# A list scheduler's table of priorities: own rows for odd quads in the middle and for the last quad

## The chip, the cores and the metric

The kernel runs on one core of one Trainium2 chip. The time is the device time in microseconds (us) of one execution. The kernel before takes 765.96 us (median of 3 runs, 761.38 to 770.71).

The engines are TensorE (PE in the profile; PEld is its weight load), VectorE (DVE), ScalarE (ACT), GpSimd (POOL) and SyncE (SP, which issues all the DMAs here). Each has a queue of its own and executes it in order. What one engine needs from another it waits for with semaphores.

## The reference

The input `x` is 128 sequences of 64 tokens of 256 numbers. One block of a hyperbolic transformer is applied to it, with a condition of 256 numbers for each sequence, and the input is added to the result:

```
ada = t_emb @ w_ada + b_ada                      # six rows of 256 for each sequence
sh_msa, sc_msa, g_msa, sh_mlp, sc_mlp, g_mlp = split(ada, 6)
xm  = expmap0(layer_norm(logmap0(x)) * (1 + sc_msa) + sh_msa)
q, k, v = plin(xm, w_q, b_q), plin(xm, w_k, b_k), plin(xm, w_v, b_v)   # to 16 heads of 16
out_h = expmap0(softmax(qt @ kt / sqrt(16)) @ vt)                      # qt = logmap0(q), ...
attn_t = g_msa * logmap0(plin(_from_heads(out_h), w_o, b_o))
x1  = mobius_add(x, expmap0(attn_t))
xm  = expmap0(layer_norm(logmap0(x1)) * (1 + sc_mlp) + sh_mlp)
ff  = plin(plin(xm, w_f1, b_f1), w_f2, b_f2)                           # 256 -> 1024 -> 256
return x + mobius_add(x1, expmap0(g_mlp * logmap0(ff)))
```

`plin(x, w, b)` is `expmap0(logmap0(x) @ w + b)`. `logmap0`, `expmap0` and `mobius_add` scale rows by factors made from norms and inner products of rows. All is float32.

## The kernel before

**Tiles and stages.** The 8192 tokens are 64 tiles of 128 rows (two sequences in each). Four tiles make a *quad*, and there are 16 quads, 0 to 15. They are worked in groups: quad 0 alone, then the pairs 1 and 2, 3 and 4, up to 13 and 14, then quad 15 alone. For each group the kernel goes through attention of its quads (`attention`, in two pairs of tiles a quad: `attention_pair`), the scalar factors of the Möbius addition (`scalars`), the inner sums and the second norm (`inner`), the MLP of its quads (`mlp`) and, a group later, the final sum and the store (`final`). The MLP has no activation function between its two matrices, so both are multiplied into one at the start (`wm`).

**Names that the prediction uses.** In attention: `yTa` are the transposed modulated rows, `fia` holds the inverse norms of a quad and `rTa` its transpose, which brings the bias into the projection; `usq` and `vsq` are squares of the projections, `qx` and `kT` transposed queries and keys, `pt` the exponentials. In the MLP: `n2s` and `n2o` are scale and shift of the second norm, `ym` the modulated rows (multiplied with `mdm` and summed with it, one half of a quad at a time), `yTm` their transpose, `fim` and `rTm` the inverse norms and their transpose, `iv` and `rTh` those of the second product; `p` is a gated product (`p<-bank,fh,gm`) and `jd` the discarded output of an inner product that is made beside it. `ja` is the discarded output of ScalarE's sums of squares. `bank` is one of the 8 banks of the matmul accumulator.

**The order is not the program's.** The code above only records operations. `Plan.add` (line 152) notes each with its engines (some may run on either of two), an estimated duration, what it reads and writes, and a *key*; `Plan.run` (line 209) then plays the machine: whenever an engine is free, it takes the operation with the smallest key among those whose inputs are there and whose buffers have room, and moves the estimated clock on. `Plan.issue` (line 381) emits the operations in that order, and the chip's queues execute what stands there. So the order of each engine's queue, the buffer that an operation gets and, where two engines are allowed, the engine are all decided by the keys and the estimates.

**The keys.** An operation's key is the number of its quad (plus 0.5 for the second half of an attention and for the group's scalars) plus an offset for its *stage*, a short name such as `qkv`, `rTa` or `mum`. The offsets stand in a table written out by hand, `pl.off`, in units of quads: -4 pulls a stage four quads ahead, 9 puts it off by nine. The stage's name gets a mark by the quad: `<` below key 3, `>` from key 13 on, none between them. A stage without an entry for its mark takes the one without a mark.

```
op.st = self.st + ("<" if self.key < self.early else ">" if self.key >= self.late else "")
op.key = (self.key + self.off.get(op.st, self.off.get(self.st, 0.0)), len(self.ops))
```

**Dummies and holds.** Where TensorE has nothing ready in the planner's clock, the planner puts a matmul of the identity with itself (`warm`, line 1373; line 1374 in the profile), which writes into a free bank that nobody reads. It does so only if TensorE's planned work in the last 2.6 us is at most `share` of them; `fill_occ`, 0.22 us, is what a dummy counts there. `hold` (line 1441) lets an engine leave a ready operation where it is, if one with a smaller key becomes ready within that many microseconds.

## Time and profile before

| | before |
|---|---|
| median of 3 runs | 765.96 us (761.38 to 770.71) |
| the profiled execution's time | 766.87 us |
| its span, first to last instruction | 765.1 us |
| mean granted TensorE clock | 0.986 |
| PE, DVE, ACT, POOL busy | 721.8, 656.1, 505.8, 122.7 us |
| read from and written to HBM | 77.89 MB, 9.18 MB |

The busy times are of one profiled execution, by engine. PE's includes the dummies of line 1374. A group of instructions is told by line, engine, operation and tiles; where a helper records every operation of a kind, all of them have its line (509 for matmuls, 516 for transposes, 449, 438 and 415 for VectorE, 492 for ScalarE), so the tiles tell them apart. Rows of stages have a stretch in us from the span's start, its length, the busy time and the number of instructions of PE, PEld, DVE, ACT and POOL, the granted clock, the busy share of the DMA engines and GB/s.

### The profile page before, as it was taken

Reading aid. Unit: us, or ns where it says so; the run is one execution under the profiler, and the core shown is the slowest. Engines: PE = TensorE matmul, PEld = TensorE weight load, DVE = VectorE, ACT = ScalarE, POOL = GpSimd, SP = SyncE. Lnnn points to the kernel's source line nnn. Section 1 sums busy time; section 2 is a strip of 40 time slices with the busy share of each in tenths; the row PEclk is TensorE's granted clock in tenths of the full one; section 3 lists DMA queues with packets and bytes.
Section 4 is the critical chain, followed back from the end, with each engine's and each line's share of the span. In section 5 each row is a group of like instructions: output and inputs, shape, how many; then the busy total and the mean of one; then the engine's idle time right before and its main releaser. Section 6 shows DMA issues by size and latency. Waiting matters only on the chain.

```text
span 765.1 us, 24046 instructions
## 1 busy us (share of the span) xinstructions
PE 721.8 (94%) x9170; PEld 513.1 (67%) x9170; DVE 656.1 (86%) x2870; ACT 505.8 (66%) x1599; POOL 122.7 (16%) x98
## 2 busy tenths in 40 slices
PE   7999999999999989998999989998999989998998
PEld 2546566676767666766867676766777666777778
DVE  6797899889987798969977898879995998989976
ACT  1345558466975879577775888487774877486453
POOL 0002102001220123002220223004310122004012
PEclk9999999999999999998899999999999999999999
DMA  5859835302560147312562157213651224126213
GB/s 157 264 146 243 192 89 152 102 29 85 146 159 30 44 126 220 90 65 74 165 165 70 57 139 201 77 57 105 169 170 30 71 73 139 56 57 159 91 45 123
DMA packets 74776, 88.63 MB, mean 116 GB/s; under 512 B 7186, under 2 KB 57630, under 8 KB 74660
## 3 DMA queue, kind: packets, MB, share of 16 engines
q1 hardware_dynamic: 74660, 87.09, 40.7%
q8 instruction: 72, 1.18, 0.7%
q14 instruction: 44, 0.36, 0.2%
HBM read 77.89 MB, written 9.18 MB: 114 GB/s over the span
## 4 chain that ended last, share of the span: by engine, by line
DVE 42%; PE 36%; ACT 10%; DMA 7%; issue 4%; POOL 1%; SPq 1%; DVEq 0%; POOLq 0%; ACTq 0%
PE bank L509 28%; ACT ja L492 6%; PE bank L516 5%; DVE x L449 5%; DVE jd L449 4%; DVE hs L464 3%; DVE u L438 3%; PE bank L1374 3%; DVE p L449 3%; DMA xp<-in_x_dram 2%; DMA mdm<-ada_d 2%; DMA gm<-ada_d 2%; DVE mxq L438 1%; ACT ym L428 1%; DVE ya L438 1%
## 5 line engine op out<-in xcount | busy, mean ns | idle before, releaser
L509 PE MATMUL bank<-wqkv,yTa 128*128 128x512 f32 (+1 forms) x512 | 177.5, 493 | 1.5 <-ACT pt L492 0.6
L509 PEld LDWEIGHTS bank<-wqkv,yTa 128*128 128x128 f32 x512 | 94.3, 191 | 72.1 <-issue 60.9
L509 PE MATMUL bank<-wm,yTm 128*128 128x256 f32 (+1 forms) x512 | 104.3, 356 | 0.5 <-DVE u L438 0.5
L509 PEld LDWEIGHTS bank<-wm,yTm 128*128 128x128 f32 x512 | 87.5, 190 | 18.8 <-issue 4.0
L441 POOL TENSOR_TENSOR x<-x,xr 128x512 f32<-128x512 f32 x31 | 40.4, 1320 | 297.4 <-ACT x L492 284.8
L1374 PE MATMUL bank<-ident 128*128 128x128 f32 x500 | 70.5, 290 | 3.0 <-ACT ja L492 1.1
L441 POOL TENSOR_TENSOR ya<-ya,mda 128x512 f32<-128x512 f32 x30 | 39.5, 1322 | 206.5 <-DMA ga<-ada_d 56.0
L509 PEld LDWEIGHTS bank<-ve,pt 64*64 64x64 f32 x4096 | 64.4, 137 | 11.2 <-issue 4.0
L492 ACT ACTIVATE pt<-bank 128x512 f32<-128x512 f32 x128 | 67.6, 606 | 5.5 <-PE bank L509 5.4
L1374 PEld LDWEIGHTS bank<-ident 128*128 128x128 f32 x500 | 63.3, 199 | 10.3 <-issue 3.7
L509 PE MATMUL bank<-ve,pt 64*64 64x17 f32 x4096 | 67.6, 209 | 0.1
L441 POOL TENSOR_TENSOR ym<-ym,mdm 128x512 f32<-128x512 f32 x31 | 42.1, 1368 | 133.6 <-DVE ym L438 48.2
L509 PE MATMUL bank<-wo,zT 128*128 128x256 f32 x256 | 60.5, 379 | 0.0
L509 PEld LDWEIGHTS bank<-wo,zT 128*128 128x128 f32 x256 | 46.2, 190 | 5.0
L492 ACT ACTIVATE qx<-bank,par 128x512 f32<-128x512 f32 x64 | 43.2, 686 | 9.1 <-PE bank L516 9.0
L516 PE MATMUL bank<-ident,u 128*128 128x128 f32 x256 | 38.7, 285 | 9.6 <-ACT pt L492 9.3
L492 ACT ACTIVATE ja<-x 128x256 f32<-128x256 f32 x64 | 26.7, 417 | 29.9 <-DVE x L449 28.9
L509 PEld LDWEIGHTS bank<-qx,kT 32*64 32x64 f32 x2048 | 32.1, 133 | 17.2 <-issue 5.6
L516 PEld LDWEIGHTS bank<-ident,u 128*128 128x128 f32 x256 | 29.2, 143 | 20.6 <-ACT pt L492 11.2
L509 PE MATMUL bank<-qx,kT 32*64 32x128 f32 x2048 | 40.4, 283 | 1.9 <-ACT qx L492 1.3
L438 DVE TENSOR_TENSOR u<-bank,g 128x512 f32<-128x512 f32 x64 | 41.5, 681 | 0.0
L449 DVE SCALAR_TENSOR_TENSOR p<-bank,fh,gm 128x256 f32<-128x256 f32 x64 | 28.1, 477 | 14.7 <-PE bank L509 11.0
(276 smaller groups left out, 1531.3 us busy)
## 6 DMA issues: line engine op xcount, KB each, us to landing
mdm<-ada_d SPq DMA_DIRECT2D x64, 256.0 KB
mda<-ada_d SPq DMA_DIRECT2D x60, 256.0 KB
x<-in_x_dram SPq DMA_DIRECT2D x16, 512.0 KB
ga<-ada_d SPq DMA_DIRECT2D x64, 128.0 KB
gm<-ada_d SPq DMA_DIRECT2D x64, 128.0 KB
xr<-in_x_dram SPq DMA_DIRECT2D x32, 256.0 KB
out_dram<-p SPq DMA_DIRECT2D x15, 512.0 KB
xp<-in_x_dram SPq DMA_DIRECT2D x26, 256.0 KB
```

The source lines that it names most:

```text
L428: fn2 = lambda: self.nc.scalar.activation(R(out), R(in0), AF.Identity, scale=R(s1), bias=R(s2))
L438: fn = lambda: self.nc.vector.tensor_tensor(R(out), R(a), R(b), op)
L441: fn2 = lambda: self.nc.gpsimd.tensor_tensor(R(out), R(a), R(b), op)
L449: fn = lambda: self.nc.vector.scalar_tensor_tensor(R(out), R(a), R(s), R(b), op0, op1, **({} if accum is None else {"accum_out": R(accum)}))
L464: fn = lambda: self.nc.vector.tensor_reduce(R(out), R(a), AX.X, ALU.add)
L492: fn = lambda: self.nc.scalar.activation(R(out), R(a), func, scale=R(scale), **{k: R(v) for k, v in kw.items()})
L509: fn = lambda: self.nc.tensor.matmul(R(out), lhsT=R(lhsT), rhs=R(rhs), start=start, stop=stop, skip_group_check=onto)
L516: fn = lambda: self.nc.tensor.matmul(R(out), lhsT=R(a), rhs=ident, start=start, stop=True, is_transpose=True, skip_group_check=not start)
L1374: nc.tensor.matmul(place[:, 0:P], lhsT=ident, rhs=ident, start=True, stop=True)
```

## The change

The marks become five. Below key 3 it is still `<`. Between 3 and 13, a key whose quad is odd (3, 5, 7, 9, 11, and their halves) gets `+`; an even one has none. From 13 to 15 it is `>`, and from 15 on, the last quad, `!`. The table of offsets is written anew as a whole, with rows for the new marks; the offsets of the old marks are other numbers too. The `share` goes from 0.92 to 0.91, PE's hold from 0.21 to 0.24 us and DVE's (in the first 60 us) from 0.06 to 0.10 us. No operation is added to the recorded program and none is taken out.

```
-        self.early, self.late = 3, 13
+        self.early, self.late, self.end = 3, 13, 15
...
-        self.span_, self.share, self.fill_occ = 2.6, 0.92, 0.22
+        self.span_, self.share, self.fill_occ = 2.6, 0.91, 0.22
...
-        op.st = self.st + ("<" if self.key < self.early else ">" if self.key >= self.late else "")
+        k = self.key
+        mid = "+" if k % 2 >= 1 else ""
+        op.st = self.st + ("<" if k < self.early else mid if k < self.late else ">" if k < self.end else "!")
...
     pl.off = {
-        "<": -4, "ada": -4, "ada<": -3.08, "ada>": 2.13, "adm": 2.82, "adm<": -3.5, "adm>": 3.3, "av": -0.83,
...
-        "kT": -3.96, "kT<": 0.62, "kT>": -3.84, "lx": -2.01, "lx<": 2.19, "lx>": 7, "md<": 6.42, "mda": 2.83,
...
+        "<": -3.58, "ada": 0.69, "ada!": 2.91, "ada+": 2.16, "ada<": 3.65, "ada>": -3.83, "adm": 8.95,
...
+        "pgm!": 2.79, "pgm+": 8.99, "pgm<": 8.97, "pgm>": 3.61, "qkb": 6.55, "qkb!": 1.04, "qkb+": 4.17,
+        "qkb<": 0.64, "qkb>": 3.27, "qkv": 8.18, "qkv!": 8.53, "qkv+": 8.21, "qkv<": 3.54, "qkv>": 8.89,
+        "qx": 6.22, "qx!": 4.12, "qx+": 4.31, "qx<": 1.44, "qx>": 3.46, "rTa": 3.09, "rTa!": 6, "rTa+": -0.02,
...
     }
...
-    pl.hold = {"PE": (0.21, 9999.0), "DVE": (0.06, 60.0)}
+    pl.hold = {"PE": (0.24, 9999.0), "DVE": (0.1, 60.0)}
```

More of the change, by code (lines that the diff above doesn't have):

```diff
@@ L600 @@
     pl.off = {
-        "<": -4, "ada": -4, "ada<": -3.08, "ada>": 2.13, "adm": 2.82, "adm<": -3.5, "adm>": 3.3, "av": -0.83,
-        "av<": -1.25, "av>": 8.97, "bx": 3.02, "bx<": -2.11, "bx>": 7.71, "by": -2.78, "by<": -3.95,
-        "by>": 5.66, "bz": 8.53, "bz<": 8.95, "bz>": 4.19, "ch": 4.71, "ch<": -1.69, "ch>": -3.61, "ex": -3.21,
-        "ex<": 1.13, "ex>": 5.07, "fya": 1.6, "fya<": 5.89, "fya>": 1.21, "fym": 4.69, "fym<": 1.69,
-        "fym>": 1.55, "ga": 9, "ga<": 7.89, "ga>": 6.71, "gm": -3.95, "gm<": 5.45, "gm>": -3.66, "hc": 0.95,
@@ L606 @@
-        "hc<": 1.15, "hc>": -3.47, "hm": 4.63, "hm<": 2.94, "hm>": -1.21, "hmb": -1.52, "hmb<": -3.47,
-        "hmb>": -3.33, "hw": -3.69, "hw<": -4, "hw>": 3.82, "hwb": 8.93, "hwb<": -3.78, "hwb>": 8.8,
-        "kT": -3.96, "kT<": 0.62, "kT>": -3.84, "lx": -2.01, "lx<": 2.19, "lx>": 7, "md<": 6.42, "mda": 2.83,
-        "mda<": 8.74, "mda>": -0.74, "mdm": 0.88, "mdm<": 2.02, "mdm>": 7.48, "moa": -0.87, "moa<": -4,
-        "moa>": -1.45, "mom": -2.58, "mom>": -3.42, "mua": 2.2, "mua<": 8.31, "mua>": -0.04, "mum": 3.37,
@@ L611 @@
-        "mum<": -3.89, "mum>": 2.67, "n1": 3.93, "n1<": 0.66, "n2": 3.18, "n2<": 1.15, "n2>": -3.63,
-        "nh": -2.81, "nh<": 6.01, "nh>": 5.74, "pga": 2.66, "pga<": -3.5, "pga>": 0.48, "pgm": 1.55, "pgm<": 9,
-        "pgm>": 2.83, "qkb": 2.71, "qkb<": -0.06, "qkb>": 2.2, "qkv": 8.94, "qkv<": 2.08, "qkv>": 8.9,
-        "qx": 6.42, "qx<": -3.88, "qx>": -4, "rTa": -3.98, "rTa<": -0.21, "rTa>": 8.73, "rTh": 5.96,
-        "rTh<": -0.68, "rTh>": 4.44, "rTm": -1.36, "rTm<": -1.12, "rTm>": 3.28, "re": 1.7, "re<": -1.82,
@@ L616 @@
-        "re>": 2.26, "sc": 6.12, "sc<": 0.63, "sc>": -2.79, "sq": 2.58, "sq<": 2.81, "sq>": 3.6, "sua": 2.79,
-        "sua<": 6.42, "sua>": 6.89, "sum": -2.26, "sum<": -3.28, "sum>": 8.47, "tpa": 7.11, "tpa<": 0.27,
-        "tpa>": 8.79, "tpm": 4.21, "tpm<": 7.83, "tpm>": -2.58, "tq": 8.33, "tq<": 6.62, "tq>": 1.73,
-        "tz": -2.84, "tz<": 4.77, "tz>": -4, "us": -1.44, "us<": -0.37, "us>": -2.96, "ve": 5, "ve<": 2.59,
-        "ve>": 5.34, "wm<": 8.98, "wp": 3.39, "wp<": 0.96, "wp>": 3.98, "x1": 3.79, "x1<": -0.25, "x1>": 0.46,
@@ L621 @@
-        "xr": 3.99, "xr<": 3.09, "xr>": 3.28, "xsa": 8.18, "xsa<": 7.52, "xsa>": -2.82, "xsm": 7.6,
-        "xsm<": 5.93, "xsm>": 3.38, "yTa": 7.23, "yTa<": 7.21, "yTa>": 8.02, "yTm": 2.78, "yTm<": -2.79,
-        "yTm>": 6.07, "yya": 8.65, "yya<": 2.22, "yya>": 3.16, "yym": 5.09, "yym<": 3.04, "yym>": 6.49,
-        "z": -0.95, "z<": 2.2, "z>": -0.13, "zT": 2.22, "zT<": 3.74, "zT>": 8.71,
+        "<": -3.58, "ada": 0.69, "ada!": 2.91, "ada+": 2.16, "ada<": 3.65, "ada>": -3.83, "adm": 8.95,
+        "adm!": 3.56, "adm+": 9, "adm<": 3.84, "adm>": 7.51, "av": 3.92, "av!": 3.64, "av+": 2.38, "av<": 0.24,
@@ new lines @@
+        "av>": 7.56, "bx": 7.53, "bx!": 8.07, "bx+": 4.33, "bx<": 3.84, "bx>": -1.16, "by": 4.82, "by!": -2.21,
+        "by+": 0.04, "by<": 6.37, "by>": 2.25, "bz": 8.88, "bz!": 4.2, "bz+": 8.99, "bz<": 8.36, "bz>": -2.47,
+        "ch": 2.74, "ch!": -3.96, "ch+": 3.28, "ch<": 3.86, "ch>": -3.77, "ex": -3.75, "ex!": 1.09,
+        "ex+": -2.24, "ex<": -3.57, "ex>": 3.48, "fya": 2.5, "fya!": 0.89, "fya+": 0.07, "fya<": -2.69,
+        "fya>": -3.11, "fym": 5.18, "fym!": -2.94, "fym+": 3.09, "fym<": -0.02, "fym>": 1.25, "ga": -0.68,
@@ new lines @@
+        "ga!": 8.32, "ga+": 9, "ga<": 8.2, "ga>": 8.13, "gm": 1.71, "gm!": -0.9, "gm+": -0.2, "gm<": 5.86,
+        "gm>": -0.17, "hc": -0.11, "hc!": -1.59, "hc+": -1.18, "hc<": -0.02, "hc>": -3.96, "hm": 2.56, "hm!": 8,
+        "hm+": 1.14, "hm<": 2.76, "hm>": -0.03, "hmb": 0.26, "hmb!": -0.23, "hmb+": 0.67, "hmb<": 3.47,
+        "hmb>": 3.07, "hw": 2.34, "hw!": 4.56, "hw+": -4, "hw<": 2.69, "hw>": 7.85, "hwb": 2.18, "hwb!": 5.15,
+        "hwb+": 6.46, "hwb<": -4, "hwb>": 8.87, "kT": -3.12, "kT!": -3.98, "kT+": -3.71, "kT<": -1.45,
@@ new lines @@
+        "kT>": 3.11, "lx": -2.8, "lx!": -3.37, "lx+": 0.29, "lx<": 6.68, "lx>": 4.97, "md<": 1.05, "mda": 8.92,
+        "mda!": -4, "mda+": 9, "mda<": 8.96, "mda>": 0.87, "mdm": 1.72, "mdm!": 7.09, "mdm+": 2.64,
+        "mdm<": -3.47, "mdm>": 6.75, "moa": -1.33, "moa!": -2.87, "moa<": -3.62, "moa>": -2.7, "mom": 3.05,
+        "mom!": -3.19, "mom>": -2.05, "mua": 1.41, "mua!": -1.44, "mua+": 1.05, "mua<": 8.62, "mua>": -2.44,
+        "mum": 0.43, "mum!": 5.25, "mum+": 5.14, "mum<": -0.55, "mum>": -0.35, "n1+": 2.93, "n1<": -0.79,
@@ new lines @@
+        "n2": 3.32, "n2!": -2.58, "n2<": 0.97, "n2>": -2.79, "nh": -1.58, "nh!": 8.87, "nh+": -1.6, "nh<": 5.81,
+        "nh>": 2.75, "pga": 5.24, "pga!": 5.81, "pga+": 2.61, "pga<": 1.27, "pga>": -1.34, "pgm": 5.81,
+        "pgm!": 2.79, "pgm+": 8.99, "pgm<": 8.97, "pgm>": 3.61, "qkb": 6.55, "qkb!": 1.04, "qkb+": 4.17,
+        "qkb<": 0.64, "qkb>": 3.27, "qkv": 8.18, "qkv!": 8.53, "qkv+": 8.21, "qkv<": 3.54, "qkv>": 8.89,
+        "qx": 6.22, "qx!": 4.12, "qx+": 4.31, "qx<": 1.44, "qx>": 3.46, "rTa": 3.09, "rTa!": 6, "rTa+": -0.02,
@@ new lines @@
+        "rTa<": 0.52, "rTa>": 4.84, "rTh": 5.4, "rTh!": 2.26, "rTh+": 8.22, "rTh<": -2.3, "rTh>": 3.16,
+        "rTm": -3.19, "rTm!": 2.65, "rTm+": -2.2, "rTm<": 3.83, "rTm>": 4.7, "re": 1.71, "re!": 8.73, "re+": 6,
+        "re<": -1.15, "re>": 0.39, "sc": 7.9, "sc!": -2.03, "sc+": 8.93, "sc<": 3.2, "sc>": 2.84, "sq": 3.69,
+        "sq!": 7.7, "sq+": 4.71, "sq<": 3.04, "sq>": 1.03, "sua": 5.55, "sua!": 3.21, "sua+": 3.09,
+        "sua<": 4.25, "sua>": 9, "sum": 0.05, "sum!": 7.17, "sum+": 4.36, "sum<": -4, "sum>": 5.2, "tpa": 5.52,
@@ new lines @@
+        "tpa!": 4.24, "tpa+": 4.96, "tpa<": 0.34, "tpa>": 8.46, "tpm": 7.26, "tpm!": -3.44, "tpm+": 3.19,
+        "tpm<": 8.43, "tpm>": -0.41, "tq": 6.57, "tq!": -3.92, "tq+": 6.16, "tq<": 6.75, "tq>": -0.7,
+        "tz": 0.34, "tz!": 5.18, "tz+": 5.26, "tz<": 5.9, "tz>": 2.71, "us": -0.62, "us!": -1.02, "us+": -2.68,
+        "us<": -2.18, "us>": -4, "ve": 7.54, "ve!": 8.92, "ve+": 5.09, "ve<": 1.33, "ve>": 7.5, "wm<": 9,
+        "wp": 6.42, "wp!": 7.08, "wp+": 5.89, "wp<": 2.13, "wp>": 8.51, "x1": 3.81, "x1!": -2.48, "x1<": 0.2,
@@ new lines @@
+        "x1>": 3.91, "xr": 3.01, "xr!": 7.7, "xr+": 0.03, "xr<": -0.76, "xr>": 8.51, "xsa": 5.05, "xsa!": -3.77,
+        "xsa+": 8.3, "xsa<": 7.15, "xsa>": -3.23, "xsm": 7.5, "xsm!": 6.59, "xsm+": 0.82, "xsm<": 5.59,
+        "xsm>": 3.57, "yTa": 4.98, "yTa!": 8.94, "yTa+": 8.8, "yTa<": 8.59, "yTa>": 6.48, "yTm": 2.72,
+        "yTm!": 1.16, "yTm+": -0.67, "yTm<": -2.34, "yTm>": 8.8, "yya": 4.73, "yya!": 5.7, "yya+": 4.83,
+        "yya<": 5.98, "yya>": 5.4, "yym": 5.49, "yym!": -1.39, "yym+": 4.99, "yym<": -0.15, "yym>": 6.65,
@@ L625 @@
+        "z": -3.31, "z!": 2.38, "z+": -1.02, "z<": 4.43, "z>": 4.12, "zT": 4.86, "zT!": 8.33, "zT+": 0.93,
+        "zT<": 4.16, "zT>": 8.43,
     }
```

## The prediction

> **What bounds the kernel now.** I read the page's busy shares and the chain that ended last, then one table of stages with the boundaries set at one recurring VectorE reduction, then the same table for the dummy matmuls alone.

> ```profile
> PE 721.8 (94%) x9170; PEld 513.1 (67%) x9170; DVE 656.1 (86%) x2870; ACT 505.8 (66%) x1599; POOL 122.7 (16%) x98
> ...
> DVE 42%; PE 36%; ACT 10%; DMA 7%; issue 4%; POOL 1%; SPq 1%; DVEq 0%; POOLq 0%; ACTq 0%
> ...
> L1374 PE MATMUL bank<-ident 128*128 128x128 f32 x500 | 70.5, 290 | 3.0 <-ACT ja L492 1.1
> ```

> TensorE looks full, but 70.5 us of its 721.8 are the 250 dummy matmuls of line 1374 (two records each, so 0.282 us a dummy) that the planner puts where TensorE would have nothing to do. Real TensorE work is 651.3 us, VectorE work 656.1 us, and the chain alternates between them: no engine bounds the whole, the order does. The stage table shows where it loses.

> ```profile
> 175.60:258.73 83.13, 80.98 (x993) 57.39 (x991) 71.01 (x300) 61.79 (x194) 13.37 (x10) 1.00 0.38 103
> 258.73:342.01 83.28, 79.45 (x1092) 56.03 (x1090) 71.61 (x305) 62.35 (x197) 15.75 (x12) 1.00 0.40 116
> 342.01:428.08 86.07, 82.95 (x1090) 59.87 (x1090) 71.45 (x303) 62.20 (x196) 15.80 (x12) 0.94 0.39 112
> 660.00:748.00 88.00, 80.46 (x782) 65.87 (x778) 78.02 (x432) 52.90 (x186) 14.54 (x12) 0.98 0.30 83
> ```

> Columns: stretch, length, busy time of PE, weight loads, DVE, ACT, POOL, then clock and DMA. The dummies alone, same stretches (PE, weight loads, clock):

> ```profile
> 175.60:258.73 83.13, 5.27 (x36) 4.43 (x36) 1.00 0.38 103
> 258.73:342.01 83.28, 3.58 (x20) 2.64 (x20) 1.00 0.40 116
> 596.00:660.00 64.00, 4.49 (x28) 3.74 (x28) 1.00 0.34 98
> 660.00:748.00 88.00, 29.48 (x226) 27.85 (x226) 0.98 0.30 83
> 748.00:765.10 17.10, 14.15 (x124) 13.96 (x124) 0.98 0.32 104
> ```

> A pair of quads in the middle takes 83.3 us, of which 79.45 - 3.58 = 75.9 us is real TensorE work: at most 7 us a pair to win. The last 105 us hold 43.6 us of dummies: the loss is at the end. There VectorE sets the pace first, and then a serial chain:

> ```profile
> 688.00:705.00 17.00, 15.89 (x126) 14.32 (x125) 16.59 (x70) 12.04 (x43) 9.35 (x8) 1.00 0.57 148
> 705.00:722.00 17.00, 14.74 (x89) 11.47 (x87) 16.46 (x114) 6.51 (x28) 0.54 (x1) 1.00 0.44 131
> 722.00:735.00 13.00, 12.29 (x73) 9.76 (x74) 9.94 (x38) 8.87 (x31) 1.59 (x1) 1.00 0.17 42
> ```

> VectorE is 97% busy from 688 to 722 us, when it delivers the normalising scale of the last quad (n2s, 722.07 us); from there the last quad's MLP runs alone and every engine waits in turn.

> **The change, part by part.** The work stays: matrix work, DMA issues (381 on SP) and ScalarE's count (one more, 1218) are the same; only the order moves. I compare the two orders by engine and price every instruction by the mean time of its form in this trace.

> Dummies: 250 become 234. At 0.282 us that is -4.5 us, but their place matters, so by stretch. Up to the attention of quad 4 there are 7 fewer, nearly all from the stretch at 175.6 us (5.27 us / 18 = 0.293 us each): -2.0 us. VectorE's order agrees: 1.9 us of its work has moved behind that point. In each of three later pairs there are 2 more, in the turn from the MLP's transposes to the next projection (3.58 / 10 = 0.36 us each, +0.7 us a pair), while VectorE's work per pair falls by 0.6 us. From there to the last output projection (686.07 us in this trace) 11 more: 4.49 / 14 = 0.32 us each, +3.5 us. Behind it 26 fewer: the 43.6 us of the last two rows are 175 dummies, 0.249 us each, so -6.5 us. Those last two together are the end: -3.0 us by TensorE.

> The end by VectorE: quads 13 and 14 now go through their MLP together and the gating products of both come later. Work ahead of n2s falls from 628.6 to 623.9 us, and as VectorE is full there, n2s comes 4.7 us earlier. But the eight instructions that leave for later now stand between the last quad's first and second modulation product: four p (28.1 us / 64 = 0.44 us) and four jd (0.42 us), 3.4 us; behind them wait this quad's second half, its squares on ScalarE and its transposes. Net -1.3 us. Eight more of the kind follow, before the small chain that makes the inverse norm; VectorE had 1.65 us of idleness at that place (728 us), which covers half: if none is covered, the end is +2.1 us instead. The ends for this term are -6.5 (the 11 late dummies only fill waits that are there anyway) and +2.1; I take -3.0, the row of TensorE's own count.

> The middle: odd quads have their own offsets there. In the repeated pair the transpose of the odd quad's inverse norms (rTa, fed by fia) moves ahead of a projection and a transpose group on TensorE; its copy moves from VectorE to ScalarE; one square stands ahead of the exponentials and one behind.

> ```profile
> 461.00 2.75 PE L509 MATMUL bank<-wqkv,yTa 128*128 128x512 f32 x8
> ...
> 463.71 0.21 DVE L415 TENSOR_SCALAR fia<-cfai 128x128 f32<-128x128 f32 x1
> ...
> 469.68 1.43 PE L516 MATMUL bank<-ident,ym 128*128 128x128 f32 x8
> ...
> 471.19 1.13 PE L509 MATMUL bank<-wqkv,yTa 128*128 128x512 f32 x2
> ```

> TensorE would reach the moved rTa at 461.0 us, where the projection starts now. fia is ready at 463.9 us today; VectorE's new order has it about 2.1 us earlier by work, at 461.8. TensorE then waits 0.8 to 0.9 us, with the projection and the transposes queued behind it. What hides it is the turn between 469.68 and 471.19 us, where TensorE waits for the copy yTm anyway (1.51 us for transposes that take 1.04 elsewhere in this trace, so 0.5 us), and the two new dummies there (0.7 us); without that cover it costs its 0.9 us a pair. ScalarE's own run to the exponentials grows by a copy (0.27) and a square (0.6) and loses a square (0.48): +0.4 us. So per pair between -0.6 us (VectorE's count) and +1.3 us (both waits uncovered); I take 0, as the engines' counts have opposite signs. Over five pairs the ends are -3.0 and +6.5 us.

> The rest: the holds that let TensorE and VectorE wait on purpose grow from 0.21 to 0.24 and 0.06 to 0.10 us in the planner; no row shows one, and what they do is already in the order. SP issues the same loads; the last quad's modulation rows go ahead of two residual loads, POOL does 29 of the ya sums instead of 30 and VectorE one more (0.69 us). VectorE's total falls by 1.0 us.

> Sum: -2.0 + 0 - 3.0 = -5.0 us on a span of 765.1, hence 760.1, and 761.9 with the 1.8 us around it (766.87 - 765.1). The median of the three runs is 0.9 us below the profiled one: **761.0 us**.

> [...] The clock first:

> ```profile
> 355.00:358.33 3.33, 1.41 (x61) 1.10 (x45) 3.33 (x17) 1.66 (x5) 0.00 (x0) 1.00 0.49 149
> 358.33:368.57 10.24, 10.24 (x214) 9.36 (x214) 7.26 (x30) 7.59 (x22) 1.26 (x1) 0.50 0.25 84
> ```

> After a stretch with 1.92 us of TensorE waiting, the granted clock was 0.50 for 10.24 us, and that pair took 86.07 us where its neighbour took 83.28: one such episode costs some 2.8 us. [...]

> **Rivals.** (1) The end gives all that its dummies say: head -2.0, end -6.5, middle -0.6 x 3 = -1.8 us: -10.3, **755.7 us**. For it: VectorE is 97% busy just where work leaves. Against it: the 11 dummies that come back before, and the 3.4 us put into the last quad's way. (2) Nothing: the waits stay and only their filling changes, or an episode at half clock eats the gain: **766 us**. (3) Slower. One mechanism, TensorE's in-order queue at the moved rTa of each odd quad: if fia doesn't come earlier on the chip (it is the tail of a chain of small VectorE instructions and two of ScalarE), TensorE stands from 461.0 to 464.0 us, 3.0 us with 2.75 us of projection behind it, in five pairs: +15.0 - 5.0 = +10.0 us, **771 us** from the median, and with one episode more 773.8. It takes the gain away from 1.0 us a pair on, and costs over 1% from 2.5 us on. For it: TensorE's share of the chain lies right behind that place. Against it: the copies and small steps that feed fia were moved earlier with it, and the turn at 469.68 with its two dummies takes up the first 1.2 us. That the change does nothing is excluded by the orders: the engines' lists differ from the start.

> **How the numbers follow.** Forecast, a gain of 2 to 10 us: 0.52, and 0.17 of it lies beyond 1%. Rival 1: 0.19, faster. Rival 2: 0.09, same. Rival 3: 0.20, slower or, for the smaller half of its waits, same (0.02). 1% (7.7 us) is about what a measurement of this kernel can tell from no change: its three runs span 761.38 to 770.71. So faster 0.36, within 1% 0.46, slower 0.18. Range: from rival 1 less the 5 us by which a run can lie under another's median, 750.5, up to rival 3's 771: 750 to 771. What is left out: the rest of rival 3 and one run in twenty below.

> **What would show it.** Right: 234 dummies (468 records), a stretch per middle pair within 1 us of 83.3 at full clock, TensorE's wait at rTa under 1 us, n2s of the last quad 4 to 7 us earlier, and less than 37 us of dummies behind the last output projection. Wrong: waits of the transposes of fia for VectorE of 2 us or more in five pairs (rival 3), a gap of 3 us and more between the last quad's two modulation products that pushes the transposes behind it later than before, or more than 21 us at half clock in all (this trace has 20.5 within the kernel).

## The result and the profile after

The changed kernel takes **774.09 us** (median of 6 runs, 770.82 to 774.86) and the kernel before, on the same chip, 763.01 (761.38 to 770.71). The ratio is **1.0119, 95% interval 1.0088 to 1.0149**: slower by over 1%, where 761.0 was predicted. Measured a second time, against 25 runs of the kernel before, it took 769.85 us (10 runs), ratio 1.0052 (1.0013 to 1.0091). Slower both times; the two intervals barely touch, and that turned out to be part of the answer.

The page of the changed kernel, its profiled execution of 770.82 us and span of 769.0 us: busy times, then the chain that ended last, then the dummies.

```profile
PE 722.5 (94%) x9138; PEld 514.0 (67%) x9138; DVE 651.4 (85%) x2870; ACT 506.9 (66%) x1600; POOL 120.4 (16%) x97
...
PE 48%; DVE 34%; ACT 8%; DMA 5%; issue 4%; SPq 1%; POOL 1%; DVEq 0%; ACTq 0%; POOLq 0%
...
L1391 PE MATMUL bank<-ident 128*128 128x128 f32 x468 | 67.7, 294 | 4.3 <-ACT ja L494 3.4
```

The work is as foreseen: 468 dummy records, 234 dummies. VectorE is busy 4.7 us less than before (1.0 us was foreseen). TensorE, though it issues 32 matmul records fewer, is busy 0.7 us *more*, and its share of the chain went from 36% to 48%. A lower clock fits that: 0.978 against 0.986. The stage table (stretch, length, then PE, weight loads, DVE, ACT, POOL, clock, DMA) has the three repeated pairs in its first rows and the end behind them:

```profile
258.07:341.79 83.72, 79.69 (x1096) 56.55 (x1094) 71.89 (x304) 63.37 (x199) 15.57 (x12) 1.00 0.40 115
341.79:431.15 89.36, 83.44 (x1094) 60.24 (x1094) 71.91 (x302) 63.28 (x198) 15.48 (x12) 0.94 0.38 108
431.15:515.53 84.38, 80.88 (x1094) 57.97 (x1094) 71.60 (x302) 63.23 (x198) 15.49 (x12) 0.98 0.41 114
...
688.00:705.00 17.00, 14.65 (x99) 12.37 (x97) 16.41 (x102) 13.59 (x54) 5.12 (x4) 1.00 0.55 134
705.00:722.00 17.00, 13.59 (x80) 11.59 (x81) 16.38 (x97) 4.91 (x18) 5.19 (x4) 1.00 0.33 102
722.00:735.00 13.00, 11.01 (x76) 8.51 (x75) 11.78 (x47) 10.17 (x38) 1.27 (x1) 1.00 0.33 102
```

A pair at full clock takes 83.72 us, where before had 83.28. The second takes 89.36 against 86.07, 3.3 us more at the same granted clock of 0.94. Where this pair ran at full clock throughout, the traces of the experiments below give it 84.47 and 84.89 us in after's order (e9, e15) and 82.99, 83.15 and 84.29 in before's (e2, e4, e13). So only some 1.2 of the 3.3 us are there without half clock; the 10.24 us at half clock cost this pair 4.5 to 4.9 us in after's order, and 2.9 to 3.1 (1.8 against e13) in before's. The two sums of waits for DMA in that stretch show one thing that is new (columns: us in total, times, longest); the first row is before's, the second after's:

```profile
DVE ym L438 <- DMA mdm<-ada_d: 1.7, 2, 0.9
```

```profile
DVE ym L440 <- DMA mdm<-ada_d: 2.9, 1, 2.9
```

And TensorE now stands at most 0.5 us at the moved `rTa`: the wait that rival 3 was made of is not there.

**How the clock is counted below.** In the profiled execution after, 34.1 us run at half clock; before, 20.5 us, and 0.6 more at its very end. The clock granted in these two traces is 1.00 or 0.50 and nothing between. Every run tells its mean granted clock, so the time at half clock is 2 x (1 - clock) x 766 us. A least-squares line over the runs that the comparisons count, one level for each kernel and one slope for all, gives 450 +- 23 us per 1.00 of clock, that is **0.29 us of time for each us at half clock**. The traces say the same without a fit: before's repeated pair has 86.07 us with 10.24 us at half clock, and its two neighbours 83.13 and 83.28: 0.28. (The comparisons, and all means below, leave out runs more than 1.5% above the fastest of their kernel, 4 of 12 in e1 and 3 of 10 in e6 among them; with these, e1's mean is 769.4 us and e6's 767.8.) By this line the difference of the means, 771.6 us after (16 runs) and 765.10 before (154 runs), falls in two: 12.2 us more at half clock, x 0.29 = **3.6 us**, and a **rest of 2.9 +- 0.5 us** at equal clock. One price for all half clock is an average: by the second pair, where it costs more in after's order, a part of the rest may be the clock's too.

### The profile page after: what moved, and what is told of

The parts are those of the page before. It is cut to its first block, busy times and chain, and to the rows that moved or that the text cites. A ratio compares the mean times of both kernels' runs of the same rounds, so it can differ in the third digit from the quotient of the medians.

```text
span 769.0 us, 23983 instructions
## 1 busy us (share of the span) xinstructions
PE 722.5 (94%) x9138; PEld 514.0 (67%) x9138; DVE 651.4 (85%) x2870; ACT 506.9 (66%) x1600; POOL 120.4 (16%) x97
## 4 chain that ended last, share of the span: by engine, by line
PE 48%; DVE 34%; ACT 8%; DMA 5%; issue 4%; SPq 1%; POOL 1%; DVEq 0%; ACTq 0%; POOLq 0%
PE bank L511 37%; PE bank L518 7%; DVE x L451 4%; ACT ja L494 4%; DVE jd L451 4%; PE bank L1391 4%; DVE p L451 3%; DVE hs L466 3%; DVE u L440 2%; DMA mdm<-ada_d 1%; DVE z L440 1%; DVE mxq L440 1%; DMA xp<-in_x_dram 1%; DMA mda<-ada_d 1%; DVE ya L440 1%
## 5 line engine op out<-in xcount | busy, mean ns | idle before, releaser
L511 PEld LDWEIGHTS bank<-ve,pt 64*64 64x64 f32 x4096 | 66.5, 141 | 12.9 <-issue 6.3
L1391 PE MATMUL bank<-ident 128*128 128x128 f32 x468 | 67.7, 294 | 4.3 <-ACT ja L494 3.4
L511 PE MATMUL bank<-ve,pt 64*64 64x17 f32 x4096 | 69.7, 212 | 0.3 <-issue 0.3
L1391 PEld LDWEIGHTS bank<-ident 128*128 128x128 f32 x468 | 60.4, 202 | 11.4 <-ACT ja L494 4.2
L466 DVE TENSOR_REDUCE hs<-usq 128x64 f32<-128x1024 f32 x32 | 38.7, 1210 | 2.0 <-ACT usq L494 1.9
```

The costliest lines, as they stand in the source:

```text
L466: fn = lambda: self.nc.vector.tensor_reduce(R(out), R(a), AX.X, ALU.add)
L511: fn = lambda: self.nc.tensor.matmul(R(out), lhsT=R(lhsT), rhs=R(rhs), start=start, stop=stop, skip_group_check=onto)
L1391: nc.tensor.matmul(place[:, 0:P], lhsT=ident, rhs=ident, start=True, stop=True)
```

## The experiments

Two theories stood after the result. The *clock* theory: fewer or displaced dummies leave stretches in which TensorE does little, and the granted clock falls to 0.50 behind them, as behind the 1.41 us of work in 3.33 us in the prediction's rows. The *order* theory: the new order itself makes something late (the `mdm` rows in the second pair, the last quad's products). All experiments issue the planner's finished orders: it is run once with before's table, share and holds and once with after's; then one order is issued up to a named stage of a quad and the other goes on, or one order is issued with a few operations displaced. `False` is before's order, `True` after's.

The table comes first. "Half" is the mean time at half clock (in a difference of two kernels uncertain by some 3 us), "level" the difference to before at equal clock (us, +-0.6 to 0.8; e8 +-1.8), and "exposure" is told of below.

| | mean us | ratio to before (95%) | half | level | exposure |
|---|---|---|---|---|---|
| before | 765.10 | | 24.3 | 0 | 3.4 |
| after (16 runs) | 771.6 | 1.0119; 1.0052 | 36.5 | +2.9 | 4.8; 4.5 |
| e1 after, then before | 766.75 | 1.0025 (0.9987 to 1.0063) | 25.1 | +1.4 | 3.5 |
| e2 before, then after | 765.63 | 1.0011 (0.9979 to 1.0042) | 28.5 | -0.7 | 5.4 |
| e3 after, end of before | 772.96 | 1.0099 (1.0064 to 1.0134) | 41.4 | +2.9 | |
| e4 before, end of after | 767.82 | 1.0043 (1.0011 to 1.0074) | 22.3 | +3.3 | 2.6 |
| e6 after, square moved | 765.47 | 0.9993 (0.9951 to 1.0035) | 22.1 | +1.0 | 4.7 |
| e7 before, square moved | 764.13 | 0.9973 (0.9935 to 1.0012) | 20.4 | +0.2 | 2.1 |
| e8 after, no dummies (3 runs) | 785.28 | 1.0243 (1.0171 to 1.0315) | 120.0 | -8.0 | 14.3 |
| e9 after, 18 more | 769.78 | 1.0048 (1.0014 to 1.0083) | 36.1 | +1.2 | 2.9 |
| e18 after, 18 in the holes | 767.68 | 1.0030 (0.9992 to 1.0068) | 28.3 | +1.4 | 3.3 |
| e10 products later | 769.36 | 1.0049 (1.0014 to 1.0085) | 33.6 | +1.5 | 5.1 |
| e16 products later still | 769.95 | 1.0056 (1.0021 to 1.0091) | 33.0 | +2.3 | 4.6 |
| e15 store behind loads | 770.84 | 1.0069 (1.0034 to 1.0103) | 37.8 | +1.8 | 4.1 |
| e11 after, holes filled | 764.36 | 0.9972 (0.9938 to 1.0006) | 18.5 | +1.0 | 1.7 |
| e17 e11 and e16 | 765.77 | 1.0009 (0.9979 to 1.0039) | 15.7 | +3.2 | 1.7 |
| e12 before, holes filled | 762.30 | 0.9949 (0.9916 to 0.9981) | 7.4 | +2.2 | 0.2 |
| e13 after's head only | 765.51 | 1.0018 (0.9982 to 1.0054) | 23.7 | +0.6 | 4.0 |
| e14 e13, holes filled | 760.15 | 0.9944 (0.9912 to 0.9977) | 10.2 | -0.8 | 0.4 |

**Halves: e1 to e4, and after itself again (e5).**

```
e1  pl.splice([(orders[True], ('sc', 11.0)), (orders[False], None)])
e2  pl.splice([(orders[False], ('sc', 11.0)), (orders[True], None)])
e3  pl.splice([(orders[True], ('tpm', 15)), (orders[False], None)])
e4  pl.splice([(orders[False], ('tpm', 15)), (orders[True], None)])
```

e1: 

> The order of after on every engine up to the scores of quad 11 (about 505 us in the traces), from there the order of before; at that point both orders have issued exactly the same work, so nothing else changes. Before has a median of 763.0 us, after 774.1. Theory 1 (the clock: the middle pairs of after leave TensorE more stretches with little work, and it falls to half clock more often): 768 to 774 us, and 27 us or more at half clock in the profile. Theory 2 (the loss arises late, in the attention of quads 12 to 15 and the MLP beside it, where the order of after puts gating and transposes otherwise): 762 to 766 us, half clock about the 20.5 us of before. Theory 3 (the loss is in the last quad's MLP): 762 to 766 us too.

e2: 

> The other half: the order of before up to the scores of quad 11, from there that of after. Theory 1: 762 to 767 us, half clock under 27 us. Theory 2 and theory 3: 771 to 775 us. If the two halves add up, the losses of this one and of its opposite over 763.0 us make 11 us together.

e3: 

> The order of after up to the transposes of the last quad's MLP input (about 700 us), then that of before (the sets of issued work differ by six operations there). Theory 1 and theory 2: the whole loss and none of what the end gives back, 773 to 779 us. Theory 3: 762 to 766 us.

e4: 

> The order of before up to the transposes of the last quad's MLP input, then that of after, with the eight products of the gating between the last quad's two modulation products. Theory 1 and theory 2: within 3 us of 763.0 (the prediction's end by VectorE had -1.3 to +2.1 us for this place). Theory 3: 771 to 775 us.

e5: 

> The changed kernel itself once more, for the granted clock of its runs beside those of before on the same chip. In the runs so far the mean clock of before is 0.985 (about 23 us at half clock), that of after 0.973 (about 41 us), and over all kernels 0.01 of clock goes with 5.4 us. Theory 1 (the clock): again 0.970 to 0.976 and 772 to 775 us; at the clock of before it would be 767. Theory 2 (the order itself makes the path longer, the clock falls because of it): the time stays 8 to 10 us above before also in the runs whose clock is as high as that of before.

In the traces the first cut (the scores of quad 11) lies at 508 to 513 us and the second at some 730 us in e4 and 737 in e3, not at about 700. Neither half up to 511 us or from there on is clearly slower by itself: 1.0025 and 1.0011. After's order up to 737 us keeps the whole loss (1.0099), and before's order with only after's end has 1.0043. So the loss doesn't sit in one place, and the pieces don't add up: levels +1.4 and -0.7 for one cut, +2.9 and +3.3 for the other, against +2.9 for the whole. e4's +3.3, with less half clock than before has, is an end that is slower by itself; the eight products that e4 has more there stand behind both modulation products and their sums, not between them (the section on e10 and e16 takes this up). The time follows the half clock in part: 25.1 and 28.5 us in the halves, 41.4 in e3, but 22.3 in e4. e5 is after's own instructions: it gave the second measurement above.

**The hole ahead of the attention products: e6 and e7.** In after's pairs TensorE waits about 1.9 us behind the scores. The timeline of TensorE and then of ScalarE in the second pair (start, duration, and in brackets the idle time before and what ended it):

```profile
354.39 1.21 PE L511 MATMUL bank<-qx,kT 32*64 32x128 f32 x64
...
357.50 1.21 PE L518 MATMUL bank<-ident,u 128*128 128x128 f32 x8 [1.91 <-ACT pt L494]
```

```profile
356.46 0.42 ACT L494 ACTIVATE ja<-x 128x256 f32<-128x256 f32 x1 [2.71 <-DVE x L451]
...
356.87 2.04 ACT L494 ACTIVATE pt<-bank 128x512 f32<-128x512 f32 x4
```

ScalarE has a square queued ahead of the four exponentials; it waits for VectorE's `x`, the exponentials stand behind it, and TensorE waits for the banks that they empty. The edit moves that square behind the exponentials in four half quads; e6 in after's order, e7 in before's:

```
+        todo = self.behind(todo, (5.5, 7.5, 9.5, 11.5))   # sua behind the four ex that follow it on ScalarE
```

e6: 

> After, with one edit in four pairs: on ScalarE the square that stands right ahead of the exponentials of quads 5, 7, 9 and 11 (second half) goes behind the four exponentials. It waits for VectorE there, and TensorE stands 1.9 us for the banks of the scores in each of these pairs; the half-clock episodes at 358, 447 and 532 us each follow such a hole. Theory 1 (clock): the holes shrink to about 0.7 us, the episodes at these places go, half clock falls by 10 to 25 us and the time by 1 to 1.3 us a pair and by 3 to 8 us for the clock: 762 to 768 us. Theory 2: only the direct part, at most 4 x 1.25 us, 769 us or more; or nothing at all if the square that comes later holds up VectorE's chain.

e7: 

> The same edit in before, which has the same hole in the same four pairs (272, 355, 440 and 523 us). Theory 1: half clock falls by about 10 to 17 us (three of the four episodes within the profiled run), the time by 5 to 10 us: 754 to 759 us. Theory 2: 759 us or more.

The hole closes from 1.91 to 0.64 us (e6, TensorE):

```profile
352.38 1.21 PE L629 MATMUL bank<-qx,kT 32*64 32x128 f32 x64
...
354.23 1.14 PE L636 MATMUL bank<-ident,u 128*128 128x128 f32 x8 [0.64 <-ACT pt L612]
```

In e6 the half clock falls from 36.5 to 22.1 us and the level from +2.9 to +1.0. In before the same edit takes the second pair's waits for the exponentials from 2.8 to 1.5 us and gives 4 us less at half clock, where 10 to 17 were expected, at a level of +0.2: no longer waiting there buys nothing by itself. In after the hole costs mostly through the clock, 4.2 of the 6.2 us by the line. The traces tell how: between 260 and 540 us, 21 of the 35 stretches at half clock last 10.2 us where the square stands ahead (13 traces, without e8), and none of 7 is longer than 6.8 us where it is moved (six traces, four of them with more dummies too).

**No dummies: e8.**

```
             if x[0] is None:
                 ...
-                    out.append((None, lambda place=best[2]: self.filler(place)))
```

> After without its 234 dummy matmuls; the order of everything else and the buffers are the same. The prediction priced a dummy at 0.28 to 0.36 us of the path, with a gain for each that goes. By that price this kernel takes 705 to 715 us. Theory 1 (dummies lie in waits that are there anyway, and all they do is hold the clock): no stretch gets shorter, half clock rises from some 40 us by 20 to 60 us, and the time is 778 to 800 us. If the clock does not answer to them at all: 773 to 775 us.

TensorE has 468 records fewer and the time is 13.7 us *longer* than after's mean (three runs, +-2.1). Its page, busy times and clock in 40 slices:

```profile
PE 689.4 (88%) x8670; PEld 477.2 (61%) x8670; DVE 650.9 (83%) x2870; ACT 506.6 (65%) x1600; POOL 120.6 (15%) x97
...
PEclk9999999999999989997899959998999989979766
```

The real work of after is 722.5 - 67.7 = 654.8 us; without dummies the same matmuls take 689.4 us. 83 us more at half clock go with 13.7 us, 0.16 each and not 0.29. Either half clock beside waits, of which the end is full, costs less, or the dummies themselves cost up to 10.9 us at equal clock (level -8.0 against +2.9); this run doesn't tell which. What they buy is more than what they cost.

**18 more dummies: e9 and e18.** The end has two holes, at 626 us (TensorE waits for `z`) and at 712 us (for `iv` of quad 13). In after's trace:

```profile
624.68 0.94 PE L1391 MATMUL bank<-ident 128*128 128x128 f32 x6
...
627.45 0.79 PE L518 MATMUL bank<-ident,z 128*128 128x128 f32 x4 [1.83 <-DVE z L440]
...
708.96 2.94 PE L1391 MATMUL bank<-ident 128*128 128x128 f32 x24
...
715.29 0.32 PE L518 MATMUL bank<-ident,iv 128*104 128x128 f32 x1 [3.39 <-DVE iv L440]
```

```
e9   +        for at, n in ((('tz', 14.0), 6), (('rTh', 15), 12)):
e18  +        for at, n in ((('tz', 14.0), 6), (('rTh', 13), 12)):
```

e9: 

> After with 18 dummies more, right behind dummies that are there, at the two holes of TensorE which before does not have: 6 ahead of the output transposes of quad 14 (first half, 625.6 to 627.5 us of the profile after) and 12 ahead of the last quad's inverse norms (711.9 to 715.3 us). Theory 1 (clock): all they do is fill holes; the half clock of after (36 us over its runs so far, 23 to 25 in before) comes down by about a third of what separates them or more, 5 to 10 us, and the time by 2 to 4 us, from 771.6 (mean of its 16 runs) to 768 to 770. By the price of the prediction (0.28 to 0.36 us a dummy on the path) it rises by 5 to 6.5 us to 777.

e18: 

> After with 18 dummies more at its two own holes, both met this time: in the first such run the 12 that were meant for the hole at 711.9 us (which stands ahead of quad 13's inverse norms) lay ahead of the last quad's, at 744 us, and the hole stayed (2.7 us). Now 6 ahead of the output transposes of quad 14 and 12 ahead of quad 13's inverse norms. If these holes make a good part of the 11 us of half clock that after has above before: half clock from 36 to 26-31 us and the mean from 771.6 to 768-770 us. If not: 33 us or more and 770 us or more. By the prediction's price of a dummy: 777.

e9's 12 missed: the last quad's `rTh` is at 744 us, and the hole at 712 kept 2.68 us. e9 therefore tests only the first hole, which went from 1.83 to 1.00 us. Its mean half clock, 36.1 us, shows no gain, but it is uncertain by some 3 us, and in the profiled executions the first hole's half clock is gone: all eight traces with after's order there and the hole as it was have a stretch at half clock that begins between 619 and 635 us, and e9, e11, e17 and e18, in which it is filled, have none there (e11's at 637 us lies 16 us behind it). The 12 that missed show a price: from the last `fim` to the end it is 35.5 us in e9, e11 and e17, which have them, and 34.4 in the other traces with after's end (without e8), so 1.1 us for 12 dummies. e18 met both:

```profile
708.33 5.62 PE L1528 MATMUL bank<-ident 128*128 128x128 f32 x48
714.66 0.32 PE L629 MATMUL bank<-ident,iv 128*104 128x128 f32 x1 [0.70 <-DVE iv L551]
```

Eighteen more dummies in the queue, 24 records in a row ending right where `iv` comes, and the kernel is **3.9 us faster** than after (767.68 against 771.6, +-1.1; against the later batch of after alone 2.9 +- 1.2), with 8.2 us less at half clock, which make 2.4 of the 3.9 by the line. How the 8.2 fall on the two holes is open: after's own trace happens to have no half clock behind the hole at 712. By the prediction's price, 0.28 us each on the path, they would have cost 5.0 us.

**The eight products in the last quad: e10 and e16.** VectorE's timeline around the last quad's modulation, first after, then before:

```profile
724.45 0.68 DVE L440 TENSOR_TENSOR ym<-ym,mdm 128x512 f32<-128x512 f32 x1
725.05 1.65 DVE L451 SCALAR_TENSOR_TENSOR p<-bank,fh,gm 128x256 f32<-128x256 f32 x4
...
728.36 1.41 DVE L440 TENSOR_TENSOR ym<-ym,mdm 128x512 f32<-128x512 f32 x2
```

```profile
722.93 2.96 DVE L438 TENSOR_TENSOR ym<-ym,mdm 128x512 f32<-128x512 f32 x3
```

The four `p` and four `jd` of quad 13 do stand between the two halves, 3.3 us of them. e10 puts them behind the second product, e16 behind the sum that follows it too:

```
e10  +        at = todo.index(dve[mum[1]]) + 1                # behind the second mum of quad 15
e16  +        at = todo.index(last_adm_of_quad_15) + 1        # behind its sums as well
     +        return todo[:at] + held + todo[at:]             # held: the eight products of quad 13
```

e10: 

> After with the eight products of quad 13 (four p, four jd), which stand on VectorE between the last quad's two modulation products, behind the second. The prediction put 3.4 us on them there. If they delay the end by that, the time at equal clock falls by 2.5 to 3.4 us. If VectorE is what bounds this stretch whatever the order of its work (they only go 0.7 us further back), nothing: within 1 us at equal clock.

e16: 

> After with the eight products of quad 13 behind both modulation products and the sum that follows them on VectorE. In the run that moved them behind the second product alone, the sum stayed behind them and started only 0.6 us earlier (728.49 against 729.08 us), so it couldn't tell. Now the last quad's modulated rows are ready 3.3 us earlier. If the prediction's 3.4 us are on the path: 2 to 3.4 us less than after at equal clock, and the four inverse norms of the last quad come as much earlier. If VectorE bounds the stretch whatever comes first: within 1 us.

In e10 the second sum still stood behind them (it started at 728.49 us, after's at 729.08), so e10 could not tell. e16 could; its VectorE:

```profile
723.07 2.96 DVE L559 TENSOR_TENSOR ym<-ym,mdm 128x512 f32<-128x512 f32 x3
725.95 1.65 DVE L570 SCALAR_TENSOR_TENSOR p<-bank,fh,gm 128x256 f32<-128x256 f32 x4
...
730.86 0.87 DVE L570 SCALAR_TENSOR_TENSOR p<-bank,fh,gm 128x256 f32<-128x256 f32 x2 [1.52 <-DMA gm<-ada_d]
```

The modulated rows are ready at about 726 us, 3.7 us earlier than in after, and the last `iv` still comes at 744.82 us (after: 744.02). So which of the two pieces of VectorE's work goes first changes nothing. That doesn't take the products off the path. What the last quad's MLP needs next is `fim`, and its small chain stands on VectorE behind all sixteen products, in e16 as in after. The chain that ended last in after runs through them, and through a load of `gm` between the first and the rest:

```profile
725.13 0.80 DVE p L451 x2
725.95 0.58 SPq L529
726.58 3.21 DMA gm<-ada_d
729.92 0.87 DVE p L451 x2
...
734.93 0.33 PE bank L518
```

From the last `n2s` to the last `fim` it is 7.18 or 7.19 us in all six traces with before's order at the end, which have no product there, 10.8 to 12.1 in the nine with after's as it is (without e8), and 13.2 in e16, where the first products and the `gm` load come later. From `n2s` to the last instruction it is 42.3 to 43.7 us against 45.3 to 47.6. In e4 eight products stand there; it has 10.87 us to `fim` and the level +3.3. By these traces the sixteen products lengthen the end by some 3 us, whatever their order ahead of `fim`; a run with them behind `fim` was not made.

**The store ahead of the modulation rows: e15.** The `mdm` loads of the second pair stand behind a store in SyncE's queue.

```
+        todo = self.store_late(todo, 4, 6)     # store of quad 4 behind the four mdm loads of quad 6
```

> After with one transfer moved on SyncE: the 512 KB store of quad 4's output goes behind the four modulation loads (mdm of quad 6) that follow it. In that pair, and in no other, VectorE waits 2.6 to 3.2 us for such a load in every trace of after's order, and TensorE 1.0 to 1.6 us for the norms behind it; the pair takes 2.4 us longer than in before at equal half clock. If the store ahead of them in the queue makes the loads late: the wait falls under 1.7 us as in the other pairs, and the pair by 1 to 2.4 us (84.5 to 82.1-83.5 us where it runs at full clock). If the loads are late because the buffer they fill comes free late: no change in wait or pair.

```profile
DVE ym L556 <- DMA mdm<-ada_d: 2.2, 1, 2.2
```

The wait is 2.2 us, in the other traces with after's order here 2.2 to 3.2: the store was not what holds the rows up, and the pair did not get shorter (84.89 us at full clock, 84.47 in e9). Why they come late stays open. The wait isn't after's alone: e7, e12 and e14, before's order with the square moved, have 2.1 to 2.7 us of it in this pair, and the pair takes them only some 0.6 us longer at equal clock than before, e2 and e4. In after's trace SyncE's queue waits around there for GpSimd's `ym`, up to 4.8 us at once (before: 3.4), as if for a buffer to come free; that was not tried.

**Filling the holes: e11, e12, e17.** e11 is e6's edit, e9's dummies and four dummies ahead of the attention products of four half quads; e17 adds e16's edit; e12 is the same idea in before's order:

```
e12  +        todo = self.behind(todo, (5.5, 7.5, 9.5, 11.5))
     +        for at, n in ((('av', 5.5), 4), (('av', 7.5), 4), (('av', 9.5), 4), (('av', 11.5), 4), (('tz', 14.0), 4), (('tz', 15.5), 4)):
```

e11: 

> After with the square behind the exponentials in four pairs, four dummies more in each of these pairs ahead of the attention products, and the 18 of the run above. Theory 1: few stretches of 3.4 us are left with under 1.64 us of TensorE; half clock 12 to 20 us over its runs, mean 763 to 766. What is left above before at equal clock (about 2 us) is the order's own cost, and stays.

e12: 

> Before with the square behind the exponentials in four pairs, four dummies more in each of these pairs ahead of the attention products, and four ahead of two groups of output transposes of the last quads. Theory 1: half clock 8 to 16 us (before: 23 to 25), mean 759 to 762 against 765.5. If dummies cost their time: 24 x 0.28 = 6.7 us more.

e17: 

> After with everything: square behind the exponentials in four pairs, 34 dummies more at the holes, and the eight products behind the sum. Without the products it had a mean of 764.4 us (18 us at half clock). If they are worth their 2 to 3.4 us: 761 to 762.5; else 764 to 765. The version of before with its holes filled had 762.3.

e11 takes after's half clock from 36.5 to 18.5 us and its mean from 771.6 to 764.36, though 12 of its 34 dummies lie at the wrong place. e12 has 24 dummies *more* than before, and is faster than before (interval below 1): its half clock is 7.4 us.

```profile
PE 720.6 (95%) x9218; PEld 512.6 (67%) x9218; DVE 654.6 (86%) x2870; ACT 506.2 (67%) x1599; POOL 123.3 (16%) x98
...
PEclk9999999999999999999999999999999999999999
```

Its 17 us less at half clock should give 5.0 us and give 2.8: the dummies and the displaced square cost 2.2 at equal clock. e17 has the lowest half clock of after's family, and its level of +3.2 takes the gain back; its `fim` comes 13.4 us behind `n2s` (3.4 of them at half clock), against 11.7 in e11.

**Only the head of after: e13 and e14.**

```
e13  pl.splice([(orders[True], ('sc', 5.0)), (orders[False], None)])
e14  e13, with the two lines of e12
```

e13: 

> The order of after up to the scores of quad 5 (about 250 us), then that of before; both have issued the same work there. Split by stage at equal time at half clock, the traces so far put after 3.4 us (standard error 0.9) ahead of before at this point, 3.9 us back over the three repeated pairs that follow, and 0.4 us ahead (1.2) from there to the end. If the head's gain is real and stays: at equal clock 2.5 to 4.3 us below before, the mean about 762 if the clock is that of before. If the split is an artefact of the clock (the head's gain is only clock that was lost elsewhere): within 1 us of before at equal clock.

e14: 

> The same with the edits of the run that filled the holes of before (square behind the exponentials in four pairs, 24 dummies more): the version that the runs point to. That one had a mean of 762.3 us with 7 us at half clock. If the head's 2.5 to 4.3 us add to it: 758 to 760 us, faster than both kernels. If not: 762.

After's order up to some 257 us, then before's, is no gain that can be told from none: level +0.6. With the holes filled it is the **fastest kernel here: 759.79 us median (755.78 to 766.25), ratio 0.9944 to before**, and it beats after by 11.5 us in the means; against e12 (0.9949) it is no better.

**Where half clock begins.** In 19 traces (all but e3's) the stretches at half clock begin on a grid of 3.413 us. The six of after begin at 78.56, 160.48, 358.45, 447.19, 532.53 and 628.10 us, 24, 58, 26, 25 and 28 times 3.413 us apart. Three pairs of grid windows of after, each the one ahead and the first at half clock:

```profile
75.19:78.60 3.41, 1.34 (x11) 0.96 (x10) 2.80 (x5) 3.02 (x10) 1.41 (x2) 0.99 0.77 194
78.60:82.01 3.41, 3.41 (x6) 1.46 (x5) 2.73 (x12) 2.19 (x8) 0.12 (x1) 0.51 0.77 223
...
443.79:447.20 3.41, 1.47 (x68) 1.23 (x68) 3.41 (x18) 1.37 (x4) 0.04 (x1) 1.00 0.43 113
447.20:450.61 3.41, 3.41 (x60) 3.16 (x57) 3.36 (x16) 3.26 (x13) 0.00 (x0) 0.50 0.37 125
...
624.69:628.10 3.41, 1.58 (x15) 1.29 (x12) 3.41 (x12) 2.03 (x10) 1.89 (x2) 1.00 0.23 77
628.10:631.51 3.41, 3.41 (x19) 3.41 (x18) 3.41 (x15) 2.23 (x10) 0.94 (x1) 0.50 0.01 2
```

TensorE was busy for 1.34, 1.47 and 1.58 of 3.41 us, and the next window ran at 0.50. From 90 us on the traces have 3,552 windows at full clock. Of the 67 with less than 1.64 us of matmul time (the small attention products, 64 x 17, counted half), 61 were followed by half clock; of the other 3,485, 45 were, and 18 of those held a whole group of such products. (The bound and the halving are fitted to these windows: 1.56 to 1.64 us parts them best.) Most of the 45, those 18 among them, also held bias products, whose weights have 4 or 8 rows (`bqkv,rTa` and `bm,rTm` 4, `bm,rTh` 8); the rest lie close above the bound, at 1.66 to 1.87 us. With the bias products counted at nothing, 96 of 127 windows under 1.56 us were followed by half clock, and only 10 of some 3,430 others. I took the grid to lie anywhere with equal chance, which no run shows, and count for each trace how many windows would be under 1.64 us, as a mean over all positions of the grid: the *exposure* of the table. One trace gives it, and it goes with the mean half clock of the kernels (correlation 0.95, without e8 0.80; about 5 us at half clock for each). Kernels that lie close it doesn't order: e9 has 2.9, e18 3.3. And it counts how often half clock begins, not how long it lasts: e6 has 4.7, as after has, and 14 us less at half clock.

## Why the prediction was wrong, point by point

**The dummies' sign: the step that failed.** The prediction priced a dummy as TensorE time: -2.0 us for 7 fewer in the head, +3.5 for 11 more, -6.5 for 26 fewer at the end. The counts were right (behind the last output projection 33.70 us of dummies, before 40.58; "less than 37" was foreseen), the price was not. e8 and e18 show the other sign: taking all away costs 13.7 us, adding 18 in two holes gains 3.9. The clock stood in the prediction as a side risk, one episode more for 2.8 us, and with nothing in the sum. It was the largest term: after has 12.2 us more at half clock in the mean, 3.6 us of the 6.5; 8.2 +- 2.9 of the 12.2 go with the two holes at the end that e18 fills. The sign named as "wrong", more than 21 us at half clock, is what came: 34.1.

**The clock, one episode of 2.8 us.** The prediction's row had 1.92 us of TensorE waiting in 3.33 us ahead of 10.24 us at half clock; the prediction took that for a risk, rightly, and then let a single episode stand for it. After's trace has six stretches at half clock, and three of them follow windows with 1.34, 1.47 and 1.58 us of TensorE's work in 3.41. Such windows should have been counted over all holes and all positions of the grid.

**The middle, 0 us (ends -3.0 to +6.5).** Comparing traces stage by stage, with 0.30 us taken off for each us at half clock, the three repeated pairs are slower by 0.9, 2.3 and 0.9 us: +4.1, inside the ends. The named wait at `rTa` was covered as argued (at most 0.5 us). The largest piece, +2.3, is the second pair; at full clock it is 1.2, and the rest comes with half clock, which costs more there (4.5 to 4.9 us for 10.24 us at half clock, in before's order 1.8 to 3.1). In every trace with after's order `ym` waits there 2.2 to 3.2 us for `mdm`; the prediction said of the loads only that SyncE issues the same ones. That the wait makes the piece isn't shown: three traces of before's order with the square moved have the wait, and a pair longer by only some 0.6 us. e15 excludes the store as its cause, no more.

**The end, -3.0 us.** From the attention of quad 11 on, the same comparison gives -3.3 us up to the last quad's scores and +2.4 behind them: -0.9. `n2s` was to come 4.7 us earlier and came 1.5 later (723.60 us, before 722.07), though VectorE's work ahead of it fell by 7.2 us (624.99 to 617.80), with the 4 us lost in the middle and the half clock ahead of it. The gap between the last quad's two products came as said, 3.3 us. The prediction charged 3.4 us for these eight products and, as the far end, as much again uncovered for the next eight, +2.1 in all; it then took TensorE's count, -3.0. VectorE's count was the one that held: `fim` came 11.05 us behind `n2s` instead of 7.18, and +2.4 behind the last quad's scores is near its far end. So this step failed too: the engine whose count was taken was not the one that the last quad's MLP waits for.

**The head, -2.0 us.** The traces show -2.9; e13, which has only this part, shows no gain (+0.6). Not shown.

**What the parts don't settle.** The stages of the traces add up to about 0.3 us at equal clock, the runs to 2.9 +- 0.5. The pieces e1 to e4 don't add up either, though e1, e2 and e4 by themselves fit the stages (+1.2, -0.9 and +2.4 by the stages, +1.4, -0.7 and +3.3 by the runs); e13 and the whole don't. (e3 says little of the end: nine of the products still stand ahead of its `fim`, 11.52 us behind `n2s`.) That the clock makes about 3.6 us is shown by taking it back (e6, e11, e18); of the other 2.9 us the traces show the products ahead of the last `fim` and the second pair, and how much the head and the stretch from quad 11 on give back stays open.

**The rivals.** Rival 3 named 771 to 773.8 us, close to the result, by a mechanism that did not occur. Rival 2's clause that half clock eats the gain was the right mechanism, with too few episodes. The full-clock pair (83.72 us, within 1 of 83.3) was right. In the range, 755.7 less 5 is 750.7 and not 750.5, which nothing hangs on.

## What to carry to other kernels

Where TensorE is busy 94% of the time with waits of 1 to 3 us, as here, price an order by the clock it leaves as well as by the path: from one trace, count the stretches of 3.4 us that hold less than about 1.6 us of matmul time, at every position of the grid (61 of 67 such windows here were followed by half clock); the count tells apart only versions that lie far from each other. Put dummies where such a stretch is, behind the last work before the wait: a dummy in a wait that is there anyway cost little here (18 of them less than they gained in e18, 24 some 2 us in e12), and without any dummies e8 took 13.7 us more. And look on the neighbouring engines for one instruction that waits ahead of the ones TensorE needs: moving it closed the hole in e6, from 1.91 to 0.64 us. Work that changes places with other work is not off the path as long as both stand ahead of what the next engine waits for: look for the first instruction that is waited for, here `fim`, and count what stands ahead of it.
